# A graph and mixture-of-experts block: second layer's part added first, gates from features not normed, and the first gathers issued ahead of the list of other slots

## The chip, the cores and the metric

The kernel runs on one core of a Trainium2 chip. Times are device microseconds of one execution, from several runs of each kernel; one further execution of each was taken by the hardware profiler, and all views of the profile are of that one.

The core's engines are named as in the profile: PE is TensorE (matmuls and transposes), PEld its loading of weights, DVE is VectorE, ACT is ScalarE, POOL is GpSimd, SP is SyncE, which in this kernel only issues DMAs. Each engine takes its own instructions strictly in order; an instruction that needs another engine's result waits on a semaphore, and everything behind it on its engine waits with it.

## The reference, cut to what matters

1250 tokens of 768 features pass through a graph part and a linear attention, whose results are added to them, and then through a layer of 8 experts of which each token takes two:

```
xn = layernorm(x)
x  = x + concat(xn, gat2(gat1(layernorm(xn)))) @ Wu + bu      # graph part
       + linear_attention(xn) @ Wo + bo                        # 12 heads
xl = layernorm(x)                      # no scale, no shift
gate = xl @ Wg + bg                    # 1250 x 8
scores, idx = top_k(gate, 2)
out = x + sum over the two experts e of
          score * (gelu(xl @ W1[e] + b1[e]) @ W2[e] + b2[e])    # 768 -> 384 -> 768
```

`gat1` and `gat2` are graph attention layers with 4 heads of 192 and 2 heads of 96 features. What the change touches lies between the end of the linear attention and the first expert. The second graph layer reaches the features through the last 192 rows of `Wu`: that product, divided by the softmax's denominators, is "the second layer's part".

## The kernel before, in words

**Stages.** The program first computes the graph layers, then keys and values of the linear attention, then a loop over five pairs of 125-token tiles (about 620 to 885 us), then a stretch in which the lists for the experts are completed (885 to 915), then the eight experts (915 to 1110), and a tail with slots beyond the fixed ones (to the end). A scheduler of the language puts each engine's instructions in order when the program is built; it works from the order in the source, its own durations and the tiles' buffers. The order on each engine is then fixed.

**The loop over pairs.** For pair `p` the features `xt` of its two tiles are loaded, and the bias `bu_b` is added. `query(p + 1)` computes the next pair's queries ahead. Then come the products of both tiles with `Wu` and `Wo`, cut into quarters in the manner of Strassen: `product` (L801) issues the matmuls, `b1`, `b6`, `b7`, `b3` and `bz` are single banks of the matmul results' memory (PSUM), and `add` (L945) adds each to a half of `xt`. When a tile's last quarter is added, `finish(t, xt)` is called:

- four matmuls with the second graph layer's results (L860), each followed by a VectorE operation that scales its 384 columns and adds them to `xt` (L862);
- `xt` goes to the output in memory (L865, SyncE's DMA);
- `normalise` (L307 to L311): two `bn_stats`, `bn_aggr`, a square root on ScalarE, a reciprocal, and `xl = (xt - mean) * rs`; `xl` goes to memory as `xl_d` (L870);
- `turn` (L319, L321) transposes `xl` in two groups of three and copies each on ScalarE; six matmuls with `Wg_sb` make the gates (L875), `bg_b` is added (L878), and the gates go to memory behind the features in the same row (L880);
- the two largest gates are found by ranks (L887 to L896), and a token's place in each expert's slots comes from a matmul with a triangle of ones and one with the counts of the tiles so far, `cum` (L900);
- that place, with the expert's `base` added (L903), is split by a shift and a mask into column and row (L905 to L914), and two one-hot matmuls into the bank `inv` (L918 to L922) collect which token sits in which slot.

**Behind the loop.** `idx` (L977, L978) holds the token of each slot, 128 slots to a column, `NJ = 10` columns to an expert, of which `FIX = 3` are always done. Then follows the list of the further columns that hold any token: a matmul for the total count (L984), 16 small VectorE operations, two transposes (L1011) and their copies `v_row` and `e_row` (L1012).

**Experts.** `gather(rows, e)` fetches the three columns' rows of `xl_d` by indirect DMA from GpSimd into `xg` (L1027, 128 rows of 776 values each, three buffers). Each is transposed by six matmuls into `px`, a tile of two banks with one buffer (L1030), and copied in two halves to `xsT` (L1033); the gate of expert `e` is copied out of the row (L1036). `inner` makes the 384 hidden values (`ph`, L1046, with Gelu on ScalarE), `give` the 768 outputs (`py`, L1058), which are scaled (L1061, L1062) and added to the output in memory by indirect DMA (L1063). The rows for expert `e + 1` are gathered between `inner` and `give` of expert `e`. Weights of an expert come as two loads of 1152 KB (L695, L697) into a ring of four.

Of the kernel before, what the change touches and what calls it, by code (L numbers as in the profile page):

```python
# [27 lines left out]
F32 = mybir.dt.float32  # L28
# [12 lines left out]
KC = D // 128  # L41
# [28 lines left out]
def gps_block(ctx: ExitStack, tc: tile.TileContext, x, src, dst, norm_g, norm_b, W1, a_src1, a_dst1,  # L70
# [652 lines left out]
    with ExitStack() as rs:  # L723
# [6 lines left out]
        def numbers(shape, pattern, base, mult, name, dt=F32):  # L730
            t = rp.tile(shape, dt, name=name)
            nc.gpsimd.iota(t, pattern=pattern, base=base, channel_multiplier=mult,
                           allow_small_or_imprecise_dtypes=True)
            return t
# [17 lines left out]
        upto = numbers([128, NE, NE], [[1, NE], [-1, NE]], 0, 0, "upto")  # L752
        nc.vector.tensor_scalar(upto, upto, 0.0, None, op0=ALU.is_ge)
        row128 = numbers([PT, 128], [[1, 128]], 0, 0, "row128", F16)
        steps = numbers([128, NE, NJ - FIX], [[0, NE], [128, NJ - FIX]], 128 * FIX, 0, "steps")
        slot_row = numbers([PT, NV], [[1, NV]], 0, 0, "slot_row", F16)
        base = numbers([PT, NE], [[128 * NJ, NE]], -1, 0, "base")
        place = numbers([128, NE], [[NJ, NE]], FIX - NV, 1, "place")
        which = numbers([128, NE], [[1, NE]], 0, 0, "which")
        col = numbers([128, 1], [[0, 1]], 0, 1, "col")  # L760
# [14 lines left out]

        cum = rp.tile([PT, NT + 1, NE], F16)
# [76 lines left out]
        def finish(t, xt):  # L853
            tk = tokens(t)

            for h in range(H2):
                for k in range(2):
                    half = slice(k * 384, (k + 1) * 384)
                    ps = bank()
                    nc.tensor.matmul(ps[:PT, :384], o2T[:C2, h, tk], Wu2_sb[:, h, half], start=True,  # L860
                                     stop=True)
                    nc.vector.scalar_tensor_tensor(xt[:, half], ps[:PT, :384], rd2[:, h, t:t + 1],  # L862
                                                   xt[:, half], op0=ALU.mult, op1=ALU.add)
            for p, tt in token_rows(t):
                nc.sync.dma_start(outr[p, tt], xt[p])  # L865

            xl = rl.tile([PT, D + NE], F32, name="xl")
            normalise(xl[:, :D], xt)
# [3 lines left out]
            turn(xT, xl, mm_p, "mm", nc.scalar.copy)  # L872
# [5 lines left out]
            nc.vector.tensor_add(gate, pg[:PT, :NE], bg_b)  # L878
# [20 lines left out]
            for i, (l, r) in enumerate(((tri, sel), (ones, cum[:, t]))):  # L899
                nc.tensor.matmul(pp[:, :NE], l, r, start=i == 0, stop=i == 1)  # L900
            nc.vector.tensor_add(cum[:, t + 1], cum[:, t], sel)
            at = rl.tile([PT, NE], F32, name="at")
            nc.vector.tensor_add(at, pp[:PT, :NE], base)  # L903
            two = rl.tile([PT, 2, NE], F32, name="two")
            nc.vector.tensor_mul(two, kth, at[:, None, :].to_broadcast([PT, 2, NE]))  # L905
            both = rl.tile([PT, 2], F32, name="both")
            nc.vector.tensor_reduce(both, two, AX.X, ALU.add)
            b_i = rl.tile([PT, 2], I32, name="b_i")
            nc.vector.tensor_copy(b_i, both)
            s_i = rl.tile([PT, 2, 2], I32, name="s_i")  # L910
            nc.vector.tensor_single_scalar(s_i[:, 0], b_i, 7, op=ALU.arith_shift_right)
            nc.vector.tensor_single_scalar(s_i[:, 1], b_i, 127, op=ALU.bitwise_and)
            s_f = rl.tile([PT, 2, 2], F32, name="s_f")
            nc.vector.tensor_copy(s_f, s_i)  # L914

            for k in range(2):
                hot = rl.tile([PT, 128], F16, name="hot")
                nc.vector.tensor_scalar(hot, row128, s_f[:, 1, k:k + 1], None, op0=ALU.is_equal)  # L918
                put = rl.tile([PT, NV], F16, name="put")
                nc.vector.tensor_scalar(put, slot_row, s_f[:, 0, k:k + 1], node1[:, t:t + 1],  # L920
# [5 lines left out]
        for p in range(NT // 2):  # L926
            left, (z1, z2) = ahead
            x2 = []
            for t in (2 * p, 2 * p + 1):
# [3 lines left out]
                nc.vector.tensor_add(xt, xt, bu_b)  # L933
                x2.append(xt)
# [40 lines left out]
            finish(2 * p + 1, x2[1])  # L975
        free = rp.tile([128, NV], F32)
        nc.vector.tensor_scalar(free, inv, 0.0, nobody, op0=ALU.is_equal, op1=ALU.mult)  # L977
        nc.vector.scalar_tensor_tensor(idx[:, :NV], inv, -1.0, free, op0=ALU.add, op1=ALU.add)  # L978
        for e in range(1, 4):
# [3 lines left out]
        pt = g_p.tile([128, 2 * NV], F32, name="g")  # L983
        nc.tensor.matmul(pt[:, :NE], ones, cum[:, NT], start=True, stop=True)  # L984
        total = rp.tile([128, NE], F32)
        nc.vector.tensor_copy(total, pt[:, :NE])
        more = rp.tile([128, NE, NJ - FIX], F32)
        nc.vector.tensor_tensor(more, total.rearrange("p (e o) -> p e o", o=1).to_broadcast(
            [128, NE, NJ - FIX]), steps, op=ALU.is_gt)
        slots = rp.tile([128, NE], F32)  # L990
        nc.vector.tensor_reduce(slots, more, AX.X, ALU.add)
        cover = rp.tile([128, NE, NE], F32)
        nc.vector.tensor_mul(cover, upto, slots[:, None, :].to_broadcast([128, NE, NE]))
        end = rp.tile([128, NE], F32)
        nc.vector.tensor_reduce(end, cover, AX.X, ALU.add)
        begin = rp.tile([128, NE], F32)
        nc.vector.tensor_sub(begin, end, slots)
        nc.vector.tensor_copy(n_more, end[0:1, NE - 1:NE])
        mine = rp.tile([128, NE], F32)
        late = rp.tile([128, NE], F32)  # L1000
        nc.vector.tensor_scalar(mine, begin, col, None, op0=ALU.is_le)
        nc.vector.tensor_scalar(late, end, col, None, op0=ALU.is_le)
        nc.vector.tensor_sub(mine, mine, late)
        nc.vector.tensor_sub(place, place, begin)
        for vals, add, row in ((place, float(NV), v_row), (which, 0.0, e_row)):
            pick = rp.tile([128, NE], F32, name="pick", bufs=2)
            nc.vector.tensor_mul(pick, vals, mine)
            one = rp.tile([128, 1], F32, name="one", bufs=2)
            nc.vector.tensor_reduce(one, pick, AX.X, ALU.add)
            pr = g_p.tile([128, 2 * NV], F32, name="g")  # L1010
            nc.tensor.transpose(pr[:1, :128], one, ident)  # L1011
            nc.vector.tensor_scalar(row, pr[:1, :128], add, None, op0=ALU.add)  # L1012


    mix.close()
    sp = ctx.enter_context(tc.tile_pool(name="sp", bufs=2))
    x_p = ctx.enter_context(tc.tile_pool(name="x_p", bufs=1, space=PSUM))
# [3 lines left out]
    def gather(rows, e):  # L1021

        xT = sp.tile([128, KC, FIX * 128], F32, name="xsT")
        gates = sp.tile([128, FIX], F32, name="gates")
        for j, r in enumerate(rows):
            xg = sp.tile([128, D + NE], F32, name="xg", bufs=3)
            nc.gpsimd.indirect_dma_start(xg, None, xl_d, bass.IndirectOffsetOnAxis(r, 0))  # L1027
            px = x_p.tile([128, 2, 512], F32, name="px")
            for c in range(KC):
                nc.tensor.transpose(px[:, c // 3, (c % 3) * 128:(c % 3 + 1) * 128],  # L1030
                                    xg[:, c * 128:(c + 1) * 128], ident)
            for a in range(2):
                nc.vector.tensor_copy(xT[:, 3 * a:3 * a + 3, j * 128:(j + 1) * 128],  # L1033
                                      px[:, a, :384].rearrange("p (b n) -> p b n", b=3))
            at = slice(D + e, D + e + 1) if isinstance(e, int) else bass.ds(e + D, 1)
            nc.vector.tensor_copy(gates[:, j:j + 1], xg[:, at])  # L1036
# [32 lines left out]
    ahead = gather(fixed(0), 0)  # L1069
    for e in range(NE):  # L1070
# [65 lines left out]
```

## Time and profile before

| | us |
|---|---|
| median of 3 runs | 1147.31 |
| lowest and highest | 1145.44, 1149.77 |
| profiled execution | 1146.65 |
| its span, first to last instruction | 1144.8 |
| mean granted TensorE clock | 0.976 |

The page of the profile lists, for each engine, busy microseconds and their share of the span; then the span in 40 equal slices, a digit for each, in tenths of the slice that the engine was busy, with a row of the clock that TensorE was granted and one of the DMA engines' load. The chain of work is found by going back from the last instruction to what released it: each row gives the start, the time that it holds on the chain, the engine, what it writes, the line and the number of instructions. In the table of stages the columns are start and end, the length, then busy time (and instructions) of PE, PEld, DVE, ACT and POOL, the granted clock, the DMA share, and GB/s. A row of waits names the engine and what waits, what it waited for, the sum, the number and the longest in microseconds.

In the page's table of DMA issues an expert's weights are `w`; a tile's `xt` and `xl` go in two DMAs each, 336 KB for 112 of the 125 tokens and 39 KB for the other 13.

### The profile page before, as it was taken

The numbers are of one execution on the slowest core, as the hardware profiler recorded it, in microseconds if no ns is written. First come the engines' busy times: TensorE is split into PE (matmuls) and PEld (weight loads), VectorE is DVE, ScalarE is ACT, GpSimd is POOL, SyncE is SP. The second block draws the span as 40 slices with busy tenths as digits, with TensorE's granted clock in tenths as the row PEclk, the third lists the DMA queues.
The fourth block names the chain that finished last, engine by engine and source line by source line (L and its number), as shares of the span: only waits on it lengthen the run. The fifth ranks groups of instructions, "written<-read, shape, count | busy, mean of one in ns | idle before, by whom it ended". The sixth has DMA issues, their size and how long they took to land.

```text
span 1144.8 us, 12035 instructions
## 1 busy us (share of the span) xinstructions
PE 1046.8 (91%) x4482; PEld 700.9 (61%) x4482; DVE 705.8 (62%) x1439; ACT 347.9 (30%) x522; POOL 74.2 (6%) x98
## 2 busy tenths in 40 slices
PE   2699998999999989988999999999999499999994
PEld 2596655579696969544554556666665256666653
DVE  7866767569696967769685857566665422222210
ACT  2141114464655555174743211120200011111121
POOL 1000000000000000000000000000000212223221
PEclk9999999999999999989999999999999599999997
DMA  5015000000000000200035011112045638787543
GB/s 161 28 31 189 14 28 1 1 1 1 1 1 1 1 1 3 80 1 1 14 129 169 12 41 41 47 36 63 20 158 180 197 72 220 208 215 189 118 63 50
DMA packets 35542, 79.76 MB, mean 70 GB/s; under 512 B 7006, under 2 KB 15536, under 8 KB 35468
## 3 DMA queue, kind: packets, MB, share of 16 engines
q1 hardware_dynamic: 29868, 59.06, 16.0%
q0 software_dynamic: 5600, 19.77, 8.6%
q8 instruction: 39, 0.64, 0.2%
q14 instruction: 35, 0.29, 0.1%
HBM read 60.48 MB, written 18.34 MB: 69 GB/s over the span
## 4 chain that ended last, share of the span: by engine, by line
PE 67%; DVE 23%; DMA 3%; issue 2%; ACT 2%; SPq 0%; POOL 0%; DVEq 0%; POOLq 0%; ACTq 0%
PE s L801 16%; PE ph L1046 9%; PE mm L599 8%; PE py L1058 7%; PE mm L430 7%; DVE scr L520 6%; DVE w L540 5%; DVE w L541 5%; PE ag L553 3%; PE mm L860 2%; PE ag L575 2%; PE mm L405 2%; PE px L1030 2%; PE ec L350 1%; PE g L875 1%
## 5 line engine op out<-in xcount | busy, mean ns | idle before, releaser
L553 PE MATMUL ag<-kept,w 125*125 125x198 f32 x800 | 137.5, 333 | 5.1 <-DVE w L541 4.8
L553 PEld LDWEIGHTS ag<-kept,w 125*125 125x125 f32 x800 | 133.5, 188 | 9.0 <-DVE w L541 9.0
L1046 PE MATMUL ph<-xsT,w 128*128 128x384 f32 (+1 forms) x324 | 102.3, 478 | 2.7 <-DVE xsT L1033 2.7
L1058 PE MATMUL py<-w,hT 128*128 128x384 f32 x300 | 100.6, 486 | 0.0
L430 PE MATMUL mm<-Wg,xnT 128*125 128x400 f32 x240 | 90.1, 513 | 1.1 <-DVE xnT L321 0.6
L540 DVE TENSOR_TENSOR w<-v,w 125x1250 f32<-125x1250 f32 x60 | 86.4, 1456 | 6.6 <-ACT w L538 5.9
L599 PE MATMUL mm<-Wv_sb,xnT 128*125 128x384 f32 x240 | 85.8, 490 | 4.8 <-DVE kvacc L619 4.8
L520 DVE CUSTOM_DVE_ANT_0 scr<-ss_row,mask 125x1250 bf16<-125x1250 f32 x60 | 87.4, 1456 | 0.5 <-ACT ss_row L511 0.2
L1046 PEld LDWEIGHTS ph<-xsT,w 128*128 128x128 f32 x324 | 61.5, 201 | 42.2 <-DVE xsT L1033 3.4
L541 DVE SCALAR_TENSOR_TENSOR w<-w,AT 125x1250 f32<-125x1250 f32 x60 | 86.5, 1457 | 0.4
L539 ACT ACTIVATE v<-dn_row,sl 125x1250 f32<-125x1250 f32 x60 | 79.3, 1333 | 17.0 <-DVE w L540 16.5
L599 PE MATMUL mm<-Wk_sb,xnT 128*125 128x384 f32 x240 | 84.5, 486 | 0.0
L801 PE MATMUL s<-w,qT 128*125 128x384 f32 x240 | 83.7, 491 | 0.0
L1033 DVE COPY xsT<-px 128x384 f32<-128x384 f32 x50 | 25.5, 552 | 87.3 <-PE px L1030 87.3
L1058 PEld LDWEIGHTS py<-w,hT 128*128 128x128 f32 x300 | 55.4, 190 | 33.8
L1061 DVE TENSOR_TENSOR ys<-py,wb 128x768 f32<-128x768 f32 x25 | 23.9, 958 | 74.1 <-PE py L1058 50.8
L599 PEld LDWEIGHTS mm<-Wv_sb,xnT 128*125 128x125 f32 x240 | 42.5, 187 | 31.1 <-DVE kvacc L619 6.9
L801 PEld LDWEIGHTS s<-w,qT 128*125 128x125 f32 x240 | 43.3, 188 | 26.9 <-issue 0.2
L538 ACT ACTIVATE w<-up_row,s 125x1250 f32<-125x1250 f32 x40 | 53.3, 1331 | 17.8 <-PE ag L553 17.6
L430 PEld LDWEIGHTS mm<-Wg,xnT 128*125 128x125 f32 x240 | 42.6, 190 | 26.1 <-ACT v L367 1.3
L599 PEld LDWEIGHTS mm<-Wk_sb,xnT 128*125 128x125 f32 x240 | 42.2, 187 | 23.5 <-issue 1.7
L356 DVE TENSOR_TENSOR AT<-AT,ec 125x120 f32 x162 | 44.4, 274 | 19.8 <-PE ec L350 18.6
(296 smaller groups left out, 1466.9 us busy)
## 6 DMA issues: line engine op xcount, KB each, us to landing
w<-in_L_ffn_W_dram SPq DMA_DIRECT2D x18, 1152.0 KB
xt<-in_x_dram SPq DMA_DIRECT2D x20, 336.0 KB
wb<-in_L_ffn_b_dram SPq DMA_DIRECT2D x9, 384.0 KB
out_dram<-xt SPq DMA_DIRECT2D x10, 336.0 KB
xl_d<-xl SPq DMA_DIRECT2D x10, 336.0 KB
W_sb<-in_L_gnn_W_dram SPq DMA_DIRECT2D x1, 2304.0 KB
Wk_sb<-in_L_mix_Wk_dram SPq DMA_DIRECT2D x1, 2304.0 KB
Wv_sb<-in_L_mix_Wv_dram SPq DMA_DIRECT2D x1, 2304.0 KB
```

The lines of the kernel that those rows point to most:

```text
L356: nc.vector.tensor_add(here, here, ec[:, g])
L430: nc.tensor.matmul(ps[:PT, :2 * (CG + 2)], xnT[:, c, t * PT:(t + 1) * PT], Wg1[:, c, 2 * k:2 * k + 2].rearrange("p h c -> p (h c)"), start ...
L520: nc.vector.tensor_tensor_reduce(scr, ss_row, mask[:, t], 1.0, 0.0, ALU.mult, ALU.max, top[:, t:t + 1])
L538: nc.scalar.activation(w, up_row, AF.Exp, bias=ss[:, st:st + 1])
L539: nc.scalar.activation(v, dn_row, AF.Exp, bias=sl[:, st:st + 1])
L540: nc.vector.tensor_tensor(w, v, w, op=ALU.max)
L541: nc.vector.scalar_tensor_tensor(w, w, 2.0, AT[:, st, :N], op0=ALU.min, op1=ALU.mult)
L553: nc.tensor.matmul(ag[:, t // 2, o:o + CG], w[:, t * PT:(t + 1) * PT], gw[:, st, hd], start=st == 0 and t % 2 == 0, stop=st == NT - 1, ski ...
L599: nc.tensor.matmul(ps[:PT, :384], xnT[:, c, t * PT:(t + 1) * PT], w[:, c, half], start=c == 0, stop=c == KC - 1)
L801: nc.tensor.matmul(ps, left[:, c], right[:, c], start=start and c == 0, stop=c == n - 1, skip_group_check=True)
L1046: nc.tensor.matmul(ph[:, :n * 128], w[0][:, o:o + 128], xT[:, c, :n * 128], start=c == 0, stop=c == KC - 1)
L1058: nc.tensor.matmul(py[:, k, :384], hT[:, f, j * 128:(j + 1) * 128], w[:, o:o + 384], start=f == 0, stop=f == FC - 1)
```

## The change

1. The second layer's part is a function of its own, `second`, and is called when a tile's features are loaded and the bias is added, ahead of the tile's products.
2. `turn` takes `xt` and not `xl`. The gates are corrected afterwards: with `Wg_s` the column sums of `Wg_sb`, which one group of six matmuls makes once, gate = (mean * `Wg_s` - product) * (-rs) + `bg_b`.
3. `base` enters the count by a third matmul instead of an addition, and a place is split into row and column with one operation fewer; the columns' numbers in `slot_row` go in steps of 128.
4. The matmul of the total count stays at the loop's end; all else of the list moves behind the gathers of the first expert. Its constants and tiles come from another pool, and its transposes use a bank of `ph`.
5. `gather` issues its three indirect DMAs first. The transposes then go through single banks, three into each with one copy behind, from a pool of two.

```diff
-        base = numbers([PT, NE], [[128 * NJ, NE]], -1, 0, "base")
+        base = rp.tile([PT, NE], F16)
+        nc.gpsimd.memset(base, 0.0)
+        nc.gpsimd.iota(base[0:1], pattern=[[128 * NJ, NE]], base=0, channel_multiplier=0,
...
+        nc.gpsimd.memset(base[32:33], -1.0)
...
+        for c in range(KC):
+            nc.tensor.matmul(pf[:PT, :NE], all1, Wg_sb[:, c], start=c == 0, stop=c == KC - 1)
+        nc.scalar.copy(Wg_s, pf[:PT, :NE])
...
-        def finish(t, xt):
+        def second(t, xt):
             tk = tokens(t)
...
                     nc.vector.scalar_tensor_tensor(xt[:, half], ps[:PT, :384], rd2[:, h, t:t + 1],
                                                    xt[:, half], op0=ALU.mult, op1=ALU.add)
+
+        def finish(t, xt):
...
-            normalise(xl[:, :D], xt)
+            mv, rs = normalise(xl[:, :D], xt)
+            nrs = rl.tile([PT, 1], F32, name="nrs")
+            nc.vector.tensor_scalar(nrs, rs, -1.0, None, op0=ALU.mult)
...
-            turn(xT, xl, mm_p, "mm", nc.scalar.copy)
+            turn(xT, xt, mm_p, "mm", nc.scalar.copy)
...
-            nc.vector.tensor_add(gate, pg[:PT, :NE], bg_b)
+            off = rl.tile([PT, NE], F32, name="off")
+            nc.vector.scalar_tensor_tensor(off, Wg_s, mv[:, 0:1], pg[:PT, :NE], op0=ALU.mult,
+                                           op1=ALU.subtract)
+            nc.vector.scalar_tensor_tensor(gate, off, nrs, bg_b, op0=ALU.mult, op1=ALU.add)
...
-            for i, (l, r) in enumerate(((tri, sel), (ones, cum[:, t]))):
-                nc.tensor.matmul(pp[:, :NE], l, r, start=i == 0, stop=i == 1)
+            for i, (l, r) in enumerate(((ones, base), (ones, cum[:, t]), (tri, sel))):
+                nc.tensor.matmul(pp[:, :NE], l, r, start=i == 0, stop=i == 2)
...
-            at = rl.tile([PT, NE], F32, name="at")
-            nc.vector.tensor_add(at, pp[:PT, :NE], base)
...
-            nc.vector.tensor_single_scalar(s_i[:, 0], b_i, 7, op=ALU.arith_shift_right)
-            nc.vector.tensor_single_scalar(s_i[:, 1], b_i, 127, op=ALU.bitwise_and)
-            s_f = rl.tile([PT, 2, 2], F32, name="s_f")
-            nc.vector.tensor_copy(s_f, s_i)
+            nc.vector.tensor_single_scalar(r_i, b_i, 127, op=ALU.bitwise_and)
+            nc.vector.tensor_copy(row_f, r_i)
+            nc.vector.tensor_sub(slot_f, both, row_f)
...
                 nc.vector.tensor_add(xt, xt, bu_b)
+                second(t, xt)
                 x2.append(xt)
...
-    x_p = ctx.enter_context(tc.tile_pool(name="x_p", bufs=1, space=PSUM))
+    x_p = ctx.enter_context(tc.tile_pool(name="x_p", bufs=2, space=PSUM))
...
     def gather(rows, e):
+        got = []
+        for r in rows:
+            xg = sp.tile([128, D + NE], F32, name="xg", bufs=3)
+            nc.gpsimd.indirect_dma_start(xg, None, xl_d, bass.IndirectOffsetOnAxis(r, 0))
+            got.append(xg)
...
-        for j, r in enumerate(rows):
-            xg = sp.tile([128, D + NE], F32, name="xg", bufs=3)
-            nc.gpsimd.indirect_dma_start(xg, None, xl_d, bass.IndirectOffsetOnAxis(r, 0))
-            px = x_p.tile([128, 2, 512], F32, name="px")
-            for c in range(KC):
-                nc.tensor.transpose(px[:, c // 3, (c % 3) * 128:(c % 3 + 1) * 128],
-                                    xg[:, c * 128:(c + 1) * 128], ident)
+        for j, xg in enumerate(got):
             for a in range(2):
+                px = x_p.tile([128, 512], F32, name="px")
+                for c in range(3):
+                    o = (3 * a + c) * 128
+                    nc.tensor.transpose(px[:, c * 128:(c + 1) * 128], xg[:, o:o + 128], ident)
                 nc.vector.tensor_copy(xT[:, 3 * a:3 * a + 3, j * 128:(j + 1) * 128],
-                                      px[:, a, :384].rearrange("p (b n) -> p b n", b=3))
+                                      px[:, :384].rearrange("p (b n) -> p b n", b=3))
...
     ahead = gather(fixed(0), 0)
+    more = fp.tile([128, NE, NJ - FIX], F32)
+    nc.vector.tensor_tensor(more, total.rearrange("p (e o) -> p e o", o=1).to_broadcast(
+        [128, NE, NJ - FIX]), steps, op=ALU.is_gt)
...
```

In the changed program the lines read: `product` L813, the second layer's part L872, the gate matmuls L891, the count L920, `inv` L941, `idx` L1002, the gathers L1018, `px` L1027, its copies L1028, `ph` L1041, the list L1067 to L1091.

## The prediction

> **What bounds the kernel now.** I read the page first, for the engine that is full and where it is not.
>
> ```profile
> PE 1046.8 (91%) x4482; PEld 700.9 (61%) x4482; DVE 705.8 (62%) x1439; ACT 347.9 (30%) x522; POOL 74.2 (6%) x98
> PE   2699998999999989988999999999999499999994
> PEclk9999999999999999989999999999999599999997
> PE 67%; DVE 23%; DMA 3%; issue 2%; ACT 2%; SPq 0%; POOL 0%; DVEq 0%; POOLq 0%; ACTq 0%
> ```
>
> TensorE is busy 91% of the span and carries 67% of the chain that ended last. One late slice stands out: the 32nd digit is 4, and its clock 5. Busy time by stage (columns: PE, PEld, DVE, ACT, POOL, clock, DMA share, GB/s) puts edges on it:
>
> ```profile
> 831.00:885.00 54.00, 54.00 (x212) 32.59 (x210) 32.66 (x106) 3.90 (x10) 0.00 (x0) 1.00 0.48 163
> 885.00:915.00 30.00, 12.94 (x54) 8.53 (x52) 14.69 (x62) 1.14 (x3) 5.51 (x6) 0.61 0.65 218
> 915.00:1110.00 195.00, 195.00 (x679) 117.91 (x680) 44.00 (x86) 34.84 (x46) 52.28 (x41) 0.99 0.65 158
> ...
> 892.00:900.00 8.00, 3.71 (x19) 2.96 (x17) 4.40 (x30) 0.73 (x2) 0.00 (x0) 0.50 0.48 140
> ```
>
> In the loop over pairs of tiles (to 885) and in the experts (915 to 1110) TensorE is never idle: VectorE work added there is free while it stays covered, and TensorE work is paid in full. Between them lie 30 us with 12.94 of TensorE. The chain there:
>
> ```profile
> 885.14 0.73 PE mm L860 x2
> 886.57 1.57 PE mm L860 x4
> 888.16 0.62 DVE xt L862
> 888.78 0.94 DVE ln_st L307 x2
> 890.52 0.69 DVE xl L311
> 891.25 0.55 PE mm L319 x3
> 892.41 2.70 PE g L875 x12
> 895.33 0.23 DVE gt L887
> ...
> 900.35 0.14 DVE idx L978
> ...
> 901.83 0.39 PE g L1011
> 902.34 0.86 issue
> 903.20 4.05 DMA xg<-xl_d,idx
> 907.34 1.53 PE px L1030 x6
> 910.01 1.53 PE px L1030 x6
> 912.69 1.53 PE px L1030 x6
> 914.85 1.65 PE ph L1046 x2
> ```
>
> From the end of the last product (about 884.95) to the first expert matmul (914.85) are 29.9 us of one tile's serial work: second layer's part, norm, turn, gates, ranks, slots, list, gather, turn. GpSimd's row of waits says what the gather waited for:
>
> ```profile
> POOL xg L1027 <- PE g L1011: 293.9, 1, 293.9
> ```
>
> idx was there from 900.48 on; the gather waited until 902.2 for the list's second transpose, though it uses nothing of it.
>
> **The change, part by part.** The sum is against the profiled execution: 1146.65 us, span 1144.8. That is 0.66 below the median of the three runs (1147.31), and I carry the difference over.
>
> *Second layer's part first.* Per tile, 4 matmuls (8 records; 884.98 to 887.56 for the last tile, 2.58 us at full clock) and 4 VectorE operations of 0.62 move from behind the products to the loading of the features. For nine tiles TensorE has the same work in another place. For the last one it moves from the open stretch into the loop: the product now ends 2.58 later, but the tile's norm needs only the last half add (0.55) behind it, instead of 3.8 us of L860 and L862 (884.95 to 888.78).
>
> The new waits: TensorE issues in order, and now meets an L872 that needs a freed bank, hence VectorE to be done with the STT before it; VectorE stands behind the bias add on the features (0.95), which needs their load, which needs the landing of the out DMA that last used that buffer and the transposes that now read it. Walking the instruction order of the changed program with these rows, per odd tile, from the end P of its last product: xl ends P+4.2, bias add P+5.25, gate P+5.4, then the STTs; TensorE meanwhile has transposes, gate matmuls and a few products of the next query, and runs dry for 0.1 to 0.4 us. The features land near P+9, and are wanted at P+11.5. On SyncE the load is queued behind the out, xl and gate DMAs of the tile (2 issues, some 0.8 us, each), as now. In the first pair the eight added matmuls meet a stretch with a little idle time (19.50 busy of 20 in 640 to 660), and come out at about nothing. Bounds for the loop: 0.2 and 4 us; taken +1.0, near the lower one because the row shows 54.00 of 54 with 32.66 of VectorE, so there is slack to absorb it.
>
> *Gates from features not normed.* Per tile three small VectorE operations (0.16 to 0.2 each, nrs, off, gate) for one add. The transposes read xt instead of xl, so they start behind the last add (P+0.8) and not behind the norm. In the loop the extra 0.4 us per tile is hidden by products; on the last tile it is on the path, inside the sum below. Once: six 125x8 matmuls and a copy for Wg_s, about 0.6 us, by the gate matmuls' row (12 records 1.37), ahead of the loop, mostly in idle time: 0 to 0.6, inside the loop's +1.0.
>
> *Slots.* A third small matmul (0.17) for base replaces the add `at`, and one operation fewer follows: on the last tile 0.4 less, in the loop ten matmuls of some 0.05 to 0.1 net, again inside the +1.0.
>
> *The last tile.* P = 884.95 + 2.58 + 1.0 = 888.5. Add to 889.3; second bn_stats half to 889.8, aggregate 890.0; transposes end 889.7; the two ScalarE copies end 890.3, the root behind them 890.7; gate matmuls end 891.1 at full clock; off, reciprocal, xl (0.68), nrs, gate end 892.5, against 895.31.
>
> Here one rule bears on a row. The gate matmuls took 2.70 in the chain and 1.37 in the loop, the clock being 0.50 from 892 on, after TensorE stood still from 888.1 to 891.25. The Trainium skill, "TensorE: Matmul & The Clock Gate", Part 1, has the clock halve after an idle window of about 3.4 us and return after as much sustained work; Part 4 there says transposes do not count as work for it. The trace agrees roughly: 3.1 idle us, and 0.58 still in 914.9 to 920. With idle gaps under 1 us the changed gate matmuls stay at full clock: 1.3 us are gained, and are in the 892.5. The rule also speaks against a larger gain: behind the gates come 10 us with hardly a matmul, so px and the first 4 us of ph stay at half clock as now. If the clock stayed up, px and ph would save some 3.5 us more; I take the row.
>
> From gate to idx took 5.2 (895.31 to 900.48); 0.4 less, and list operations between: idx at 897.6 with 0.3 of slack.
>
> *List behind the gathers.* The first gather now waits for idx and not for the list; 0.86 of issue as now: 898.5 instead of 903.20. Its DMA waits, too, for the xl and gate writes, issued near 892.4 and 892.6, which is 5 us before. The list's 16 VectorE operations (about 0.2 each) and two transposes now lie in the gather's flight of 4.05 us; left over are reading of e_row and the bias copy (0.5 together) between the gather's copies. Were that cover gone, the list would cost the 1.7 us it does today. On GpSimd's queue nothing else stands behind the first three gathers: the next three wait, as now, for the buffers' transposes. The extra memset and iota for base run at the start of the stage, where GpSimd is 0% busy: nothing.
>
> *Landing.* The row gives 4.05, free of other traffic; page and trace have 3.7 to 5.8 for others. But two weight loads of 1152 KB, issued at 896.2 and 896.6, kept the DMA engines full from 898 to 904, and in the changed kernel are issued some 3 us sooner, filling 895 to 901.5: the gather moves into their end. "DMA: Bandwidth & Descriptors", Queues, rings and completion order, says that an engine takes turns between queues by packet: for an overlap of 2 us that costs up to 1 us. By the row alone landing is 902.55, by the rule 903.5; taken 903.1, and 2 us late as the bad end.
>
> *Single banks.* Gathers land at G, G+1.45, G+2.75 (issues at 903.20, 904.67, 905.94). Before, each px took two banks and waited for both copies: px started 2.67 apart (907.34, 910.01, 912.69), ph 7.5 after the first. Now the transposes of one half (0.76 at half clock) run beside the copy of the other (0.55): px 1 G to 1.6, px 2 to 3.1, px 3 from 3.5, held 0.4 by the bias copy, to 5.0; ph at G+5.0 = 908.1. In the experts the banks turn with about 0.03 us to spare behind a single py matmul, so a wait of 0 to 0.1, some 14 times: 0 to 1, taken 0.3.
>
> **Sum:** 914.85 - 908.1 = 6.75 earlier, less 0.3: 6.45. The experts are TensorE-bound (195.00 of 195) and the tail hangs on the last expert, so this reaches the end: 1140.2 for the profiled execution, 1140.9 against the median.
>
> **The rivals.**
> A, the sum above: 0.62. With its own bounds (loop 0.2 to 2.5, landing 902.5 to 904.5) 1139.5 to 1144; 1137 if the clock stayed up.
> B, the gather only waits for something else: weight loads on the same DMA engines hold all three gathers to the end of their stretch, or one late write of xl does. Then only the turn (2.5) and some 1 us are won: about 1143.5 to 1145, 0.20. For it: 1.06 of DMA in 900 to 903.2 before. Against: the loads end sooner as well.
> C, slower: the loop. TensorE waits at the L872 of the next pair because the features land late, or because the STTs stand behind norm and gates on VectorE. That is paid four times, at pairs 2 to 5. It decides from (6.75 - 0.3)/4 + 0.25 = 1.9 us per pair; the features would have to land about 4.4 us after P+9. At 3.4 us per pair the kernel is at 1153. For it: SyncE's queue also holds expert weights, and DMA share rises to 0.48 in the last pair. Against: 2.5 us of slack in the walk. 0.18 in all, of which 0.10 past 1153.
> D, that the list was not what the gather waited for, is excluded by the row of waits and by the changed program, where the gather's semaphores name idx, the inv matmul and the writes.
>
> **How the numbers follow.** About 0.5% (5.7 us) is what a measurement here tells from no change: faster means under 1141.6. Of A some six sevenths lie there (the middle of its bounds and the case of the full clock), with nothing of the rest: 0.53. B, the rest of A and the milder part of C: 0.37. C's hard part: 0.10. Range: 1136 (no loop cost, full clock in part) to 1148 (B and the mild C).
>
> **What would show it.** Right: in the pair loop TensorE idle under 0.6 us per pair, period about 54 us; gate matmuls of the last tile near 1.4 us; first gather 4.5 to 5 us ahead of 903.20 and waiting on DVE idx; px in threes, ph about 5 us behind the first landing. Wrong: rows of PE waiting on DVE at L872 or L920 above 1.9 us per pair (C); a landing over 5.5 us after issue, with the DMA full (B); py or px waiting for xsT copies by more than 0.1 us each in the experts; the last tile's gates at 2.7 us again.

## The result, and the profile after

| | before | after |
|---|---|---|
| median of 6 runs, us | 1148.05 | 1139.43 |
| lowest and highest | 1145.44, 1150.60 | 1136.18, 1142.28 |
| profiled execution, and its span | 1146.65, 1144.8 | 1136.18, 1134.2 |

The ratio is 0.9922, with a 95% interval of 0.9899 to 0.9945. A repetition later, on another occasion, gave 0.9933 (0.9920 to 0.9946). So the change brings 7.7 to 9 us. The two profiled spans lie 10.6 apart; part of that is chance, as will be seen.

First the same lines of the page as before: busy time, TensorE and its clock by slices, and the shares of the chain that ended last.

```profile
PE 1040.6 (92%) x4504; PEld 695.0 (61%) x4504; DVE 710.1 (63%) x1449; ACT 347.9 (31%) x523; POOL 75.7 (7%) x101
PE   2599998999999989988999999999999599999994
PEclk9999999999999999999999999999999799999997
PE 70%; DVE 21%; issue 2%; DMA 2%; ACT 2%; POOL 0%; DVEq 0%; POOLq 0%; ACTq 0%
```

The hole in the 32nd slice is smaller (5 for 4), and the clock in it is 7 instead of 5. The stages, in the same windows:

```profile
831.00:885.00 54.00, 53.99 (x211) 32.24 (x210) 30.21 (x100) 5.27 (x11) 0.00 (x0) 1.00 0.50 162
885.00:915.00 30.00, 18.17 (x78) 11.13 (x77) 14.48 (x68) 3.00 (x5) 5.95 (x6) 0.77 0.68 233
915.00:1110.00 195.00, 194.40 (x690) 118.94 (x688) 46.39 (x86) 34.95 (x47) 53.93 (x42) 1.00 0.65 158
```

TensorE is still busy throughout the loop, so no long wait for the moved operations stands there. The chain through the stretch:

```profile
889.45 0.54 PE mm L319 x3
889.99 1.40 PE g L891 x12
...
892.51 0.24 DVE xl L898
...
897.61 0.15 DVE idx L1002
...
898.83 5.45 DMA xg<-xl_d,idx
...
904.32 0.92 PE px L1027 x3
905.25 0.56 DVE xsT L1028
...
905.88 0.90 PE px L1027 x3
...
907.44 0.61 PE px L1027 x3
...
908.68 3.49 PE ph L1041 x10
```

No norm stands ahead of the transposes any more, the gate matmuls take 1.40 and not 2.70, the gather follows idx by 1.1, transposes and copies alternate, and the third group of transposes is already quicker (0.61 for 0.92): the clock is coming back. Set side by side, with the prediction's steps (each step from the start of one row to the start or end of the next; the first mark is the first small transpose of the stage, the last product's end is the end of its rows; "the first 36 ph" run to the start of what follows them):

| us | before | predicted | after | after, repeated |
|---|---|---|---|---|
| start to the first mark of the stage | 622.9 | 622.9 | 621.0 | 621.8 |
| to the end of the last product | 262.2 | 265.8 | 267.8 | 269.2 |
| to the last tile's gates | 10.20 | 4.0 | 3.95 | 3.96 |
| to idx | 5.18 | 5.1 | 5.01 | 5.01 |
| to the first gather's issue | 2.72 | 0.9 | 1.08 | 1.08 |
| to the first px | 4.14 | 4.6 | 5.49 | 4.95 |
| to the first ph | 7.51 | 5.0 | 4.36 | 4.43 |
| the first 36 ph | 13.85 | 13.85 | 11.72 | 11.72 |
| to the last px (the extra slot's) | 188.8 | 189.1 | 188.2 | 188.2 |
| to the end | 27.3 | 27.3 | 25.6 | 26.0 |

### The profile page after: what moved, and what is told of

Same layout as the page of the kernel before. It is cut to its first block, busy times and chain, and to the rows that moved or that the text cites. A ratio compares the mean times of both kernels' runs of the same rounds, so it can differ in the third digit from the quotient of the medians.

```text
span 1134.2 us, 12113 instructions
## 1 busy us (share of the span) xinstructions
PE 1040.6 (92%) x4504; PEld 695.0 (61%) x4504; DVE 710.1 (63%) x1449; ACT 347.9 (31%) x523; POOL 75.7 (7%) x101
## 4 chain that ended last, share of the span: by engine, by line
PE 70%; DVE 21%; issue 2%; DMA 2%; ACT 2%; POOL 0%; DVEq 0%; POOLq 0%; ACTq 0%
PE s L813 19%; PE ph L1041 8%; PE mm L599 8%; PE py L1053 8%; PE mm L430 7%; DVE scr L520 6%; DVE w L540 5%; DVE w L541 5%; PE ag L553 3%; PE mm L872 2%; PE ag L575 2%; PE mm L405 2%; DMA out_dram<-ys,idx 1%; PE px L1027 1%; PE ec L350 1%
## 5 line engine op out<-in xcount | busy, mean ns | idle before, releaser
L1041 PE MATMUL ph<-xsT,w 128*128 128x384 f32 (+1 forms) x324 | 98.6, 464 | 1.0 <-DVE xsT L1028 1.0
L1041 PEld LDWEIGHTS ph<-xsT,w 128*128 128x128 f32 x324 | 58.8, 191 | 39.3 <-DVE xsT L1028 1.5
L813 PE MATMUL s<-w,qT 128*125 128x384 f32 x240 | 82.7, 493 | 0.0
L1028 DVE COPY xsT<-px 128x384 f32<-128x384 f32 x50 | 25.8, 552 | 68.0 <-PE px L1027 67.9
L813 PEld LDWEIGHTS s<-w,qT 128*125 128x125 f32 x240 | 43.2, 188 | 28.1 <-issue 1.8
L430 PEld LDWEIGHTS mm<-Wg,xnT 128*125 128x125 f32 x240 | 42.2, 188 | 26.1 <-ACT v L367 1.4
```

Of the source, the lines that this page charges most:

```text
L430: nc.tensor.matmul(ps[:PT, :2 * (CG + 2)], xnT[:, c, t * PT:(t + 1) * PT], Wg1[:, c, 2 * k:2 * k + 2].rearrange("p h c -> p (h c)"), start ...
L813: nc.tensor.matmul(ps, left[:, c], right[:, c], start=start and c == 0, stop=c == n - 1, skip_group_check=True)
L1041: nc.tensor.matmul(ph[:, :n * 128], w[0][:, o:o + 128], xT[:, c, :n * 128], start=c == 0, stop=c == KC - 1)
```

## The experiments

All numbers of a kind in one table, from one profiled execution each; the ratio to the kernel before is that of the timed runs. "Pair" is the period of a pair of tiles in the loop, by the starts of its first `inv` matmuls. "P" is the end of the last product.

| run | ratio, 95% interval | pair | mark to P | P to gates | idx to issue | issue to px | px to ph | 36 ph | P to last px |
|---|---|---|---|---|---|---|---|---|---|
| before | | 53.79 | 262.2 | 10.20 | 2.72 | 4.14 | 7.51 | 13.85 | 232.4 |
| changed | 0.9922 (0.9899, 0.9945) | 54.46 | 267.8 | 3.95 | 1.08 | 5.49 | 4.36 | 11.72 | 219.8 |
| e1 second part back | 0.9924 (0.9886, 0.9963) | 54.35 | 265.3 | 6.99 | 1.07 | 4.87 | 4.83 | 12.22 | 223.2 |
| e2 gates back | 0.9950 (0.9930, 0.9970) | 54.29 | 267.1 | 6.86 | 1.08 | 4.07 | 5.21 | 12.48 | 222.9 |
| e3 two banks | 0.9986 (0.9968, 1.0005) | 54.46 | 269.5 | 3.95 | 1.07 | 5.20 | 7.53 | 13.56 | 225.1 |
| e4 pool only | 0.9990 (0.9975, 1.0006) | 53.78 | 263.2 | 10.55 | 1.08 | 4.54 | 7.52 | 13.91 | 231.6 |
| e5 slots back | 0.9912 (0.9856, 0.9968) | 54.32 | 266.9 | 3.95 | 1.08 | 5.12 | 4.66 | 11.71 | 219.9 |
| e6 weights early | 0.9973 (0.9958, 0.9987) | 54.47 | 268.3 | 3.95 | 4.73 | 3.91 | 5.18 | 12.81 | 223.8 |
| e7 kept warm | 0.9936 (0.9913, 0.9958) | 54.47 | 269.1 | 3.95 | 1.08 | 5.34 | 3.74 | 11.71 | 219.0 |
| e8 banks alone | 0.9966 (0.9950, 0.9983) | 53.78 | 263.7 | 10.21 | 2.72 | 4.19 | 5.06 | 11.72 | 227.3 |
| e9 last tile only | 0.9905 (0.9890, 0.9920) | 53.79 | 265.5 | 3.95 | 1.08 | 5.05 | 3.74 | 11.72 | 218.9 |
| e10 banks and pool | 0.9934 (0.9913, 0.9956) | 53.78 | 263.4 | 10.20 | 1.07 | 4.10 | 5.14 | 12.65 | 226.5 |
| e11 loop parts alone | 0.9984 (0.9974, 0.9994) | 54.47 | 268.9 | 3.95 | 2.91 | 4.22 | 7.76 | 13.51 | 226.2 |
| e12 changed again | 0.9933 (0.9920, 0.9946) | 54.46 | 269.2 | 3.96 | 1.08 | 4.95 | 4.43 | 11.72 | 219.3 |

Two of these columns say what is chance. Programs with the same loop differ by up to 1.8 us from mark to P (267.8 to 269.5 with the changed loop, 262.2 to 263.7 with the old one), by short waits in the first pair. A difference between single profiles below that says little, unless it shows in one step alone. The mark itself came between 620.3 and 625.3 in all fourteen profiles, though nothing ahead of it was touched. Both profiles that the two kernels are known by stand at the lucky end of their loops; the first changed one reached the mark early as well.

### What each part is worth: e1, e2, e5

The edits put one part of the changed kernel back.

```diff
 # e1: the second layer's part is called in finish again
                 nc.vector.tensor_add(xt, xt, bu_b)
-                second(t, xt)
...
         def finish(t, xt):
+            second(t, xt)
```

> The changed kernel with the second layer's part called at the head of finish again, behind the products; all else as changed. Serial theory: the last product ends 2.6 us sooner against the first small transpose of the stage, and 3.8 us of matmuls and VectorE stand behind it instead of one add of 0.55, so the first expert matmul comes 0.5 to 1 us later than in the changed kernel. Loop theory (the moved matmuls break up the products of the next pair and cost the 0.68 us by which each pair's period grew, 53.79 to 54.47): the period returns to about 53.8, the loop gives back 2.7 us, and the kernel ends about 2 us sooner than the changed one.

The loop became 2.5 shorter, the stretch to the gates 3.0 longer, the pair period fell by only 0.11. The serial theory is right in kind: the part is worth half a microsecond on the path to the gates, and the timed runs cannot tell it from nothing (0.9924 against 0.9922 or 0.9933). That the moved matmuls make most of the longer period is refuted.

```diff
 # e2: no column sums, gates from the normed features
-            turn(xT, xt, mm_p, "mm", nc.scalar.copy)
+            turn(xT, xl, mm_p, "mm", nc.scalar.copy)
...
-            nc.vector.scalar_tensor_tensor(gate, off, nrs, bg_b, op0=ALU.mult, op1=ALU.add)
+            nc.vector.tensor_add(gate, pg[:PT, :NE], bg_b)
```

> The changed kernel with the gates made from the normed features again (no column sums, turn reads xl, one add). Serial theory: the last tile's transposes wait for xl, TensorE is idle for some 3 us ahead of them, the gate matmuls run at half clock (2.7 us), idx comes 2.5 to 3.5 us later behind the last product, and the first expert matmul with it. Loop theory: the transposes and gate matmuls need no splitting, the pair period falls to 53.8 to 54.1 and 1.2 us of column sums go, so 2 to 4 us come back and the end moves by under 1 us.

The gates came 2.9 later, as the serial theory has it; the loop gave back less than hoped (period 0.17 shorter). The gather was issued 4.8 us behind the second weight load and not 4.1 as in the changed kernel, and reached px in 4.07. From P to the last px this kernel is 3.1 behind the changed one, in the timed runs 2 to 3 us (0.9950 against 0.9933 and 0.9922): by these single returns the largest of the three parts in front of idx.

```diff
 # e5: base added on VectorE, two count matmuls, shift and mask
-            for i, (l, r) in enumerate(((ones, base), (ones, cum[:, t]), (tri, sel))):
+            for i, (l, r) in enumerate(((tri, sel), (ones, cum[:, t]))):
...
+            nc.vector.tensor_add(at, pp[:PT, :NE], base)
```

> The changed kernel with base added on VectorE again, two matmuls for the count and the shift and mask as before. The pair period of the changed kernel is 54.47 against 53.79; putting the second layer's part back took 0.11 of the 0.68, the old gates 0.17. Splitting theory (each small matmul put between product matmuls costs time, and the count now interrupts the products twice for a tile): the period falls to about 54.1, 1.5 us come back in the loop, and idx of the last tile comes about 0.4 later; the end about 1 us sooner. Other theory (the split of turn and gate matmuls, which stays, makes the 0.4): the period stays near 54.45 and the end comes 0.4 later.

The period fell by 0.15, gates to idx rose from 5.01 to 5.18. Neither theory was quite right, and the timed runs show no difference: 0.9912, its wide interval holding the changed kernel's ratio. The three single returns take 0.11, 0.17 and 0.15 from the period, 0.43 of 0.68; all three together (e9 below, where they stay for the last tile only) take all of it.

### Banks, and the clock: e3, e8

```diff
 # e3: px over two banks, one buffer; the gathers still issued first
-    x_p = ctx.enter_context(tc.tile_pool(name="x_p", bufs=2, space=PSUM))
+    x_p = ctx.enter_context(tc.tile_pool(name="x_p", bufs=1, space=PSUM))
...
-                px = x_p.tile([128, 512], F32, name="px")
+            px = x_p.tile([128, 2, 512], F32, name="px")
```

> The changed kernel with px as one tile of two banks and one buffer again, the three gathers still issued first. Serial theory: px of the three gathers start 2.67 apart, the first expert matmul comes 7.5 instead of 4.4 us behind the first landing: 3.1 us later, and the end by as much. Clock theory: TensorE works only 1.5 of each 2.67 us, so the clock is not back when ph starts, the first 36 ph matmuls take 14.0 instead of 11.9, and the end comes 5 to 5.5 us later.

Both theories' effects came: px to ph 3.2 longer, the first 36 ph 13.56. The gathers were still issued first, so it is the banks that count here, and not that order. The ratio rose to 0.9986: without single banks the rest of the change can't be told from nothing. The other way round, e8 puts the changed `gather` into the kernel before and nothing else:

```diff
 # e8: the kernel before, gathers first, px in single banks
-    x_p = ctx.enter_context(tc.tile_pool(name="x_p", bufs=1, space=PSUM))
+    x_p = ctx.enter_context(tc.tile_pool(name="x_p", bufs=2, space=PSUM))
...
-            px = x_p.tile([128, 2, 512], F32, name="px")
+                px = x_p.tile([128, 512], F32, name="px")
```

> The kernel before with the changed gather alone: three gathers issued first, single banks of px. Clock and bank theory: the first expert matmul comes 4.4 to 5 us behind the first px instead of 7.51, the first 36 ph take 11.7 to 12.5 instead of 13.85, the experts 0.6 less: 5 to 5.5 us in all, more than half of what the whole change brings. Serial theory alone: 2.5 to 3 us.

From P to the last px it won 5.1 us, and the timed runs gave 0.9966, 4 us. The TensorE rows of its timeline (start, length, what, count, and in brackets the idle time ahead) show what TensorE then does:

```profile
907.62 1.51 PE L1035 MATMUL px<-ident,xg 128*128 128x128 f32 x6 [5.19 <-DMA xg<-xl_d,idx]
909.61 3.07 PE L1035 MATMUL px<-ident,xg 128*128 128x128 f32 x12 [0.47 <-DMA xg<-xl_d,idx]
912.68 11.88 PE L1049 MATMUL ph<-xsT,w 128*128 128x384 f32 x36
```

The transposes fill 4.6 of 5.1 us, and the 36 ph behind them take 11.88. In the kernel before, three blocks of 1.5 us with gaps of 1.2 left the clock down. Its clock column (last but two), and below it that of the changed kernel:

```profile
912.70:914.80 2.10, 1.50 (x6) 1.10 (x6) 0.71 (x3) 0.00 (x0) 0.37 (x2) 0.50 0.60 163
914.90:917.00 2.10, 2.10 (x4) 1.18 (x5) 0.52 (x2) 0.00 (x0) 0.53 (x1) 0.50 0.40 86
917.00:919.00 2.00, 2.00 (x5) 1.08 (x4) 0.15 (x1) 0.00 (x0) 0.00 (x0) 0.50 0.28 115
```

```profile
904.30:906.50 2.20, 2.17 (x9) 1.65 (x9) 1.37 (x5) 0.00 (x0) 0.37 (x1) 0.50 0.32 133
906.50:908.60 2.10, 2.06 (x11) 1.19 (x9) 1.76 (x5) 0.00 (x0) 1.50 (x2) 0.74 0.43 87
908.70:912.00 3.30, 3.30 (x10) 1.99 (x11) 0.66 (x2) 0.00 (x0) 0.95 (x1) 1.00 0.86 267
```

Before, the clock was 0.50 until 919, some 4 us after ph began. After, it came back inside the row with 0.74, by that mean at about 907.6: 3.3 us after px began, and ahead of ph. Transposes without gaps count as work for the clock here.

### What held the gather: e4

```diff
 # e4: the kernel before, the list's constants and tiles in the lasting pool
-        total = rp.tile([128, NE], F32)
+        total = fp.tile([128, NE], F32)
...
-        more = rp.tile([128, NE, NJ - FIX], F32)
+        more = fp.tile([128, NE, NJ - FIX], F32)
```

> The kernel before with one edit: the list's constants and tiles come from the pool that outlives the stage (fp), not from the one closed behind it (rp). Order and computation are as before. Memory theory: the gather waited for the list only because its buffers take over the memory of the closed pool; it then waits for idx, and is issued at about 901.4 instead of 903.2 on the scale of the profile before: 1 to 1.8 us sooner, the end too. Order theory (the list has to stand behind the gather in the program): no change, the gather still waits for the list's second transpose.

The gather came 1.08 behind idx, as in the changed kernel, though the list still stood ahead of it in the program. So the wait was one for memory: gather buffers take the place of a closed pool's tiles, and wait for their last readers, the list's transposes among them. Where the list stands does not matter. Of the 1.64 won, 0.8 were left at the last px (the landing took 0.4 longer, and the gates had come 0.35 later), which the timed runs (0.9990) don't resolve.

### The landing, and a filled gap: e6, e7

```diff
 # e6: the fourth expert's weight loads from GpSimd's queue
-        for e in range(1, 4):
+        for e in range(1, 3):
...
     ahead = gather(fixed(0), 0)
+    ring.append(expert(fW1[3], fW2[3], fb2[3], nc.gpsimd))
```

> The changed kernel with the fourth expert's two weight loads issued from GpSimd's queue, ahead of the gathers, as soon as the last product frees their buffer, and not from SyncE's queue behind the last tile's writes. Contention theory (the first gather took 5.49 us from issue to the first transpose, against 4.14 before, because it runs against the end of these loads): the loads run from about P to P+7 and are over when the gather is issued at P+10, so the first transpose comes about 4.1 us behind the issue, and all behind it 1.3 us sooner. Write theory (the loads now delay the last tile's writes, for which the gather waits): the gather is issued later than P+10, and nothing or less is won.

The write theory was right. SyncE's, GpSimd's and one of VectorE's rows of the timeline:

```profile
896.41 1.05 SPq L886 DMA_DIRECT2D xl_d<-xl  x2
897.56 0.80 SPq L900 DMA_DIRECT2D xl_d<-xl  x2
```

```profile
893.47 1.07 POOL L695 DMA_DIRECT2D w<-in_L_ffn_W_dram  x1 [280.54 <-issue]
894.53 0.82 POOL L697 DMA_DIRECT2D w<-in_L_ffn_W_dram  x1
906.46 1.04 POOL L1018 DMA_INDIRECT xg<-xl_d,idx  x1 [11.11 <-DVE bias L1113]
```

```profile
905.49 0.15 DVE L1111 COPY rows<-idx 128x1 int32 x1 [1.96 <-DMA xl_d<-xl]
```

idx was there at 901.7, and the gather went at 906.5: the writes of the last tile, issued behind the loads, kept it 3.7 us longer. (The gather's bracket names the nearest event on VectorE; that engine had itself waited for `xl_d<-xl`, until 905.49.) With the loads long over, the gather then took 3.91 to px. So the loads do cost the changed kernel's gather about 1 us (5.49 and 4.95 against 3.91 to 4.22 in e2, e6, e8, e10 and e11), but ahead of the writes they cost more.

```diff
 # e7: four matmuls into a bank that nobody reads, behind the list's transposes
+    for _ in range(4):
+        py = y_p.tile([128, 2, 512], F32, name="py")
+        nc.tensor.matmul(py[:1, 0, :384], one, ring[0][0][:, :384], start=True, stop=True)
```

> The changed kernel with four more matmuls (1x384, from the second pick and expert 0's weights, into a bank that nobody reads) behind the list's transposes, so that TensorE works through most of the gather's flight. Clock theory: the clock is back at or soon after the first px, px of the three gathers take about 0.5 instead of 0.9 a half, and the first expert matmul comes 3 to 4 us behind the first landing instead of 4.36; the first 36 ph stay at 11.7. End 0.5 to 1.3 us sooner. Copies theory (VectorE's copies and the gathers' spacing of 1.3 to 1.5 set the pace, not the transposes): ph at 4.2 or more, no gain.

px to ph fell from 4.4 to 3.74, within the 3 to 4 us that the clock theory gave. Now VectorE's copies hold TensorE:

```profile
908.81 1.01 PE L1027 MATMUL px<-ident,xg 128*128 128x128 f32 x6 [0.32 <-DVE xsT L1028]
910.00 1.01 PE L1027 MATMUL px<-ident,xg 128*128 128x128 f32 x6 [0.19 <-DVE xsT L1028]
```

In the timed runs the 0.6 us do not show (0.9936).

### Two edits, three parts, one better version: e10, e11, e9, e12

e10 joins e8 and e4. e11 is the changed kernel with e3's banks, the old `gather` and the old list: only the parts ahead of idx stay. e12 repeats the changed kernel. They shared a chip.

```diff
 # e10: the kernel before with e8's gather, and
-        total = rp.tile([128, NE], F32)
+        total = fp.tile([128, NE], F32)
...
 # e11: the changed kernel with e3's px, the old order of gathers, and
-        total = fp.tile([128, NE], F32)
+        total = rp.tile([128, NE], F32)
```

> The kernel before with two edits alone: the changed gather (single banks), and the list's tiles in the lasting pool, their order as before. Loop theory: the loop's 262 to 264 us stay, P to the last tile's gates stays at 10.2, the gather comes 1.08 behind idx instead of 2.72, the first expert matmul 4.5 to 5 behind the first px, ph at full clock: 6 to 7 us sooner than before, within 2 us of the whole change. Rival (the moved second layer's part and the gates carry most of it): under 4 us.

> The changed kernel with its list and its gather put back as before: what stays is the second layer's part ahead, gates from raw features and the slots. Loop theory: 3 us more in the loop, some 3.7 us less between last product (2.5 later) and idx, nothing at px and ph: within 1 us of the kernel before, no change that can be measured. Rival (these parts are worth what the stretch shows, 6.25 us to the gates): 3 us sooner or more.

> The changed kernel once more, unaltered, beside the others on one chip, for the comparison with them: 0.992 of the kernel before by its first result. In its profile the early stages, which nothing touches, show how much of the 10.6 us between the first two profiles belongs to the single executions: by the medians, about 2.

e10's two edits alone reach 0.9934, the changed kernel's 0.9933, and the timed runs can't tell the two apart. (In e10's profile 5.9 us are won from P to the last px; its 7.6 us in the timed runs have an interval from 5 to 10, so part of them may be chance.) e11's three parts alone reach 0.9984, 1.8 us: more than the 1 us that the loop theory allowed, less than the 3 of its rival. In the profile the three parts bring 6.25 us to the gates and take 5.6 in the loop. Of the 10.6 us between the first two profiles, e12 lets 2.2 appear as chance (the same kernel, span 1136.4).

What the parts cost is paid by ten tiles, and what they bring is brought by the last alone. e9 gives them to the last tile only (slots as before everywhere), with e7's filling.

```diff
+            last = t == NT - 1
+            if not last:
+                second(t, xt)
...
-            turn(xT, xt, mm_p, "mm", nc.scalar.copy)
+            turn(xT, xt if last else xl, mm_p, "mm", nc.scalar.copy)
...
                 nc.vector.tensor_add(xt, xt, bu_b)
-                second(t, xt)
+                if t == NT - 1:
+                    second(t, xt)
```

> A version built from the findings: the second layer's part ahead and the gates from raw features for the last tile alone, slots as before for all tiles, the list behind the gathers in the lasting pool, single banks, and the four filling matmuls of the run before. Loop theory (what the change costs the loop is paid by all tiles, what it brings is brought by the last one): pair period 53.8 instead of 54.47, the stage up to the last product 1.5 to 2.5 us shorter than changed, the stretch to the first expert matmul as changed or 0.6 shorter; the end 2 to 3 us sooner than the changed kernel. Rival (the period comes from the column sums or from the scheduler's other order): period stays above 54.3, no gain over the changed kernel but the 0.6.

The period is 53.79 again, the stretch behind P is as short as in e7, and the kernel is the fastest of all: median 1136.38, against 1139.74 for the changed kernel beside it, ratio 0.9905 (0.9890 to 0.9920) to the kernel before.

```profile
888.91 0.54 PE L319 MATMUL mm<-ident,xt 125*128 125x125 f32 x3 [0.26 <-DVE xt L970]
889.29 1.54 PE L891 MATMUL g<-Wg_sb,xT 128*125 128x8 f32 x12
898.60 4.49 PE L1099 MATMUL py<-w,one 128*1 128x384 f32 x8
903.52 0.87 PE L1032 MATMUL px<-ident,xg 128*128 128x128 f32 x6 [0.43 <-DMA xg<-xl_d,idx]
```

The last tile's gates go at full clock, and px starts at it.

## Why the prediction was right, and which steps were wrong

The time forecast (1140.9) and the direction held. Its sum is made of steps that were partly wrong in both directions. In the repeated profile the loop and the landing cost some 3.8 us more than forecast, and px to ph, the clock at ph and the experts some 3.6 less. That these nearly cancel is luck, and the close time with it.

- **The last tile and the list: right.** P to gates 3.95 (4.0 forecast), to idx 5.01 (5.1), to the issue 1.08 (0.9). The gate matmuls ran at full clock. The list, though, was not freed by its move: e4 shows that its pool was what counted.
- **The loop, +1.0: mis-sized, it is about +3** (mark to P grew by 5.6, of which 2.6 are the moved second layer's part). Rival C's waits at L872 or at the count do not appear. No long wait appears, and the work itself takes longer: a pair's period grew by 0.68 in each of the first two (over four pairs that would be 2.7), and the column sums take 1.2, less some idle time of the first pair. For the column sums the prediction put 0.6, but the row that it took this from (12 records, 1.37) is that of six such matmuls already. Counted from each TensorE record's start to the next over these two periods, a pair's products take 0.25 more, the `inv` matmuls 0.20, the second layer's part 0.09, gates and transposes 0.09, and the added count matmul 0.06. The `inv` matmuls' share is a wait too short for the view of waits. Before, in one tile of each pair, matmuls of the second layer's part stood between the two; now the second follows the first at once and starts 0.17 behind it, 0.05 after VectorE has made its `put`:

```profile
740.50 0.20 PE L922 MATMUL inv<-put,hot 125*128 125x80 f16 x1
740.54 0.88 PE L860 MATMUL mm<-Wu_sb,kept 96*125 96x384 f32 x2
741.26 0.20 PE L922 MATMUL inv<-put,hot 125*128 125x80 f16 x1
```

```profile
739.60 0.30 DVE L939 TENSOR_SCALAR put<-slot_row,slot_f,node 125x80 f16<-125x80 f16 x1
739.78 0.37 PE L941 MATMUL inv<-put,hot 125*128 125x80 f16 x2
```

  The first three rows are the kernel before, the others the changed one. For the products it is the order of the rows that differs, here around one even tile of the changed kernel:

```profile
781.95 0.49 PE L319 MATMUL mm<-ident,xt 125*128 125x125 f32 x3
782.27 0.81 PE L813 MATMUL s<-w,xnT 128*125 128x384 f32 x2
783.05 0.82 PE L891 MATMUL g<-Wg_sb,xT 128*125 128x8 f32 x6
783.72 0.89 PE L813 MATMUL s<-w,xnT 128*125 128x384 f32 x2
784.45 0.49 PE L319 MATMUL mm<-ident,xt 125*128 125x125 f32 x3
```

  and here around one of the kernel before:

```profile
838.95 0.81 PE L319 MATMUL mm<-ident,xl 125*128 125x125 f32 x6
839.59 0.81 PE L801 MATMUL s<-w,qT 128*125 128x384 f32 x2
840.24 1.37 PE L875 MATMUL g<-Wg_sb,xT 128*125 128x8 f32 x12
```

  Before, six transposes and twelve gate records stood in one group each; now they come as three and six with products between. From start to start the two product records take 0.65 before (839.59 to 840.24), and 0.78 and 0.73 after (782.27 to 783.05, 783.72 to 784.45). e9 shows that the 0.68 belong to the three parts together. How they divide among the parts is not settled, since single returns took 0.43 in sum; and the splitting of gates and transposes can't be most of it, for in e2 they stand in whole groups again and 0.50 remain.
- **Landing, 4.6: mis-sized, it is 5.0 to 5.5.** The prediction took from the Trainium skill ("DMA: Bandwidth & Descriptors", Queues, rings and completion order) that a DMA engine takes turns between queues by packet, and put 0.5 us for it; against the 4.14 of before it was 0.8 to 1.4. (That row was not free of other traffic, as the prediction had it: the DMA share was still 0.96 in 902 to 904.) Rival B was thus right in its mechanism, though far from its size.
- **px to ph, 5.0: 4.36**, because the third group of transposes was already at full clock.
- **The clock at ph: the step that failed.** I held that "px and the first 4 us of ph stay at half clock as now", after the Trainium skill ("TensorE: Matmul & The Clock Gate", Part 4), that transposes do not count as work. They do here, and the measurement decides: the first 36 ph took 11.72 and not 13.85, so 2.1 us were won that the sum did not have. (The profile names them MATMUL; whether they run in the mode of which that page speaks, no view shows.) This, and the experts (0.09 us less each; 0.3 more in sum were forecast, 0.6 less came), made up for the loop and the landing.
- **The tail, 1.7 us less, and the early stages, 1.9:** nothing of the change stands in the early stages. In the tail it is not the single banks, since with two banks it took 26.1 in e3 and 26.3 in e11. In the kernel before, and in e4 alone besides, the granted clock fell to 0.50 once more for 3.4 us of the tail (1120.6 to 1124.0 before); why there, stays open.

So what the forecast took for a gain of serial work (6.75) is for the larger part the single banks' (5.1 us in e8's profile: 2.5 by the overlap of transposes and copies, 2.1 by the clock, the rest in the experts; 4 us in its timed runs, and 6 to 7 when e3 takes them out of the changed kernel). What stands ahead of the gather won 8 us there (1.6 of them by the list's pool) and gave 5.6 of them to the loop.

## What to carry to other kernels

Where a stretch of serial work ends a loop, shorten it for the last pass alone: the same rewrite in all passes can cost a full engine nearly as much as the one pass wins. After a wait, the gaps in TensorE's first work decided here when its clock came back: feed it without gaps, by smaller buffers that turn over instead of one large one. And when an instruction waits for something that it does not use, look for the memory it takes over before moving code.

## What the runs showed of the hardware that was not expected

- Transposes bring the clock back in this kernel. By the granted clock, full speed came 3.3 us after the first px in the changed kernel (3.4 in e12, 4.2 in e5), where the transposes had no gap over 0.15 us; with gaps of 1.2 in 2.7 us it came 11.3 to 11.9 us after it, some 4 us into ph (before, e3, e4, e11). With one gap of 0.2 to 0.6 us it came after 5.0 to 7.4 (e8, e1, e2, e10, e6). The 36 ph took 11.7, 13.5 to 13.9, and 11.7 to 12.8. In e7 and e9 the filling matmuls had brought it back ahead of px.
- An engine that shows 54.00 busy of 54 can still take 0.68 us longer for nearly the same work: here about 0.2 in waits too short to be listed, 0.06 in an added matmul, and the rest in longer steps where the order of the instructions had changed.
- Three gathers of 128 rows and two loads of 1152 KB on the same DMA engines: px came 4.9 to 5.5 us behind the first gather's issue when that was 4.1 to 4.2 behind the second load's (changed, e1, e3, e5, e7, e9, e12), and 3.9 to 4.2 when it was 4.8 or more behind (before, e2, e6, e8, e10, e11); e4, with 4.9, took 4.54.
